# Gated cross-attention block with 64 routed experts: five of eight token groups' experts computed by slots instead of densely, and a new order of the attention's PE work

## The chip, the cores and the metric

The kernel runs on one core of a Trainium2 chip, in fp32. The metric is the device time of one execution in microseconds (us). The engines are PE (TensorE: matmuls and transposes, results in PSUM), DVE (VectorE), ACT (ScalarE), POOL (GpSimd, which also issues the indirect DMAs) and SP (which issues nearly all other DMAs).

## The reference

`x` is 32 batches of 128 tokens of 128 features; a context of the same shape goes with it. First a gated attention with 16 heads of 8 features is added to `x`, then a mixture of 64 experts:

```python
x = x + tanh(g_xattn) * xattn(layernorm(x), ctx)
x = x + tanh(g_ffn) * ffn(layernorm(x))

# xattn: self-attention (kind 0) and attention to ctx (kind 1), both from the queries of x
dots = einsum('bhqd,bhkd->bhqk', q, k) * scale          # scale = 1/sqrt(8)
out  = softmax(dots) @ v * (1 - gate) + softmax(dots_aux) @ va * gate
return out @ Wo + bo

# ffn: per token, 8 of 64 experts
scores = sigmoid(x @ gate_w.T); sc = scores + gate_bias
# the best 4 of 8 groups of experts by the sum of their two best sc, then the best 8 experts in them
tw = scores[chosen] / sum(scores[chosen]) * 2.5
for every expert e:   y += w_dense[:, e] * ((silu(x @ We_gate[e]) * (x @ We_up[e])) @ We_down[e])
return y + (silu(x @ Ws_gate) * (x @ Ws_up)) @ Ws_down
```

The weight of an expert that a token has not chosen is zero. Each expert has 64 hidden features.

## The kernel before

**Units and blocks.** A unit `u` is one batch with one kind of attention: 64 units. A block is 4 batches (512 tokens): 8 blocks. All expert weights stay in SBUF.

**Attention.** `prepare(a)` makes, for two batches, the normalized and transposed inputs (`tp`, `srcT`), queries and keys (`pp`, `qk`), a masked copy of each for pairs of heads (`bd`, on POOL) and the values (`vp`, `v`). For each unit, `scores_max` computes scores `sp` on PE and their negative row maxima `nm` on DVE; `queries` transposes the maxima (`nt`) and adds them to the queries (`qa`); `softmax` computes the scores a second time, transposed and shifted (`st`), and takes their exponential on ACT (`pt`); `values` multiplies with the values (`op`) and copies to `osb`. `divide` (`ot`, `rd`, `at`) and `project` (`mt`, `yp`) finish a batch. `ln_scales` gets the layer norm's inverse root by three Newton steps on DVE (L288 to L295).

**Routing.** When a block's four batches are done, `route(t)` normalizes, transposes (`xtp`, `xT`), computes the gate's scores (`lg`, `sc`), selects groups and experts on DVE, and writes the block's 64 x 512 weights transposed to DRAM (`w_dram`). It is a generator that is advanced a few steps a unit (`route_some`).

**Experts, all dense.** `pair()` takes the next pair of experts of a routed block. There are 33 a block: 32 pairs and the shared expert. `hidden(t, n)` multiplies the block's 512 tokens with gate and up weights of both experts (`gu`, two products of 128x128 with 512 columns), takes silu by Tanh on ACT and two DVE instructions (`th`), and scales by the token weights on POOL (`h`); the weights `cw` are read from DRAM, broadcast over 64 partitions, two pairs in one tile. `down` accumulates `y` over the 33 pairs in one PSUM bank, LAG = 3 pairs behind; after the last, `ysb`, `yt` add the block's sum to `x` and it is stored.

**Order.** A loop over units issues the work: `queries(u-1)`, `scores_max(u)`, a pair, `project`, `divide`, `softmax(u-1)`, a pair, a routing step, `values(u-2)`, a pair, a routing step, a pair. The tile scheduler then orders each engine's instructions; `softmax` is placed before other waiting work by `high_priority` but behind the pair's `down` (`BEHIND`). What is left of the pairs follows the loop. PSUM's eight banks: three double banks (`ps_s`) shared by `sp`, `st` and `gu`, one for everything else, one for `y`.

Of the kernel before, what the change touches and what calls it, by code (L numbers as in the profile page):

```python
# [13 lines left out]
I32 = mybir.dt.int32  # L14
AF = mybir.ActivationFunctionType
# [6 lines left out]
P = 128  # L22
# [4 lines left out]
BG = 4  # L27
# [4 lines left out]
PQ = 2  # L32
AHEAD = 60
LAG = 3
# [3 lines left out]
MAGIC = float(0x5F3759DF)  # L38
BIG = 3.0e38
EPS = 1e-5  # L40


@with_exitstack
def gated_block_kernel(
# [81 lines left out]
    wg_sb = keep.tile([P, E, F], F32, name="wg_sb")  # L126
    wu_sb = keep.tile([P, E, F], F32, name="wu_sb")
    wd_sb = keep.tile([P, NPAIR, D], F32, name="wd_sb")
    wsg_sb = keep.tile([P, F], F32, name="wsg_sb")
    wsu_sb = keep.tile([P, F], F32, name="wsu_sb")  # L130
    wsd_sb = keep.tile([F, D], F32, name="wsd_sb")

    def load_experts(e0):
        e1, p0 = e0 + 8, e0 // 2
        yield nc.sync.dma_start(
            out=wg_sb[:, e0:e1, :], in_=We_gate[e0:e1].rearrange("e d f -> d e f")
        )
        yield nc.sync.dma_start(
            out=wu_sb[:, e0:e1, :], in_=We_up[e0:e1].rearrange("e d f -> d e f")
        )  # L140
        yield nc.sync.dma_start(
            out=wd_sb[:, p0 : p0 + 4, :],
            in_=We_down[e0:e1].rearrange("(p e) f d -> (e f) p d", e=2),
        )

    def load_shared():
        yield nc.sync.dma_start(out=wsg_sb, in_=Ws_gate)
        yield nc.sync.dma_start(out=wsu_sb, in_=Ws_up)
        yield nc.sync.dma_start(out=wsd_sb, in_=Ws_down)

    weight_loads = [partial(load_experts, e0) for e0 in range(0, E, 8)] + [load_shared]

# [4 lines left out]
    nc.gpsimd.memset(one, 1.0)  # L157

# [9 lines left out]
        channel_multiplier=0,  # L168
    )
# [106 lines left out]
    def ln_stats(src, mv):  # L276
        st = work.tile([P, V.BN_STATS_DIM], F32, tag="bnst", name="bnst", bufs=4)
        V.bn_stats(st, src)
        V.bn_aggr(mv, st)

    def ln_scales(mv, n, name):


        var, rs, nr, mr = (
            work.tile([P, n], F32, tag=f"{k}{n}", name=f"{k}_{name}")
            for k in ("var", "rs", "nr", "mr")
        )
        V.tensor_scalar(var, mv[:, :, 1], EPS, None, ALU.add)  # L288
        V.tensor_scalar(rs.bitcast(I32), var.bitcast(I32), -0.5, MAGIC, ALU.mult, ALU.add)
        for _ in range(3):  # L290
            V.tensor_tensor(nr, rs, rs, ALU.mult)
            V.tensor_tensor(nr, nr, var, ALU.mult)
            V.tensor_scalar(nr, nr, -0.5, 1.5, ALU.mult, ALU.add)
            V.tensor_tensor(rs, rs, nr, ALU.mult)
        V.scalar_tensor_tensor(mr, mv[:, :, 0], -1.0, rs, ALU.mult, ALU.mult)  # L295
        return rs, mr
# [6 lines left out]
    fix = ctx.enter_context(tc.tile_pool(name="fix", bufs=1))  # L303
    lp = ctx.enter_context(tc.tile_pool(name="lp", bufs=2))
    work = ctx.enter_context(tc.tile_pool(name="work", bufs=2))
    rt = ctx.enter_context(tc.tile_pool(name="rt", bufs=1))
    hp = ctx.enter_context(tc.tile_pool(name="hp", bufs=2))

    ps_s = ctx.enter_context(tc.tile_pool(name="ps_s", bufs=3, space=PSUM))
# [9 lines left out]

    def share_banks():  # L320

        early.close()
        ps_m.append(ctx.enter_context(tc.tile_pool(name="ps_m1", bufs=1, space=PSUM)))
        ps_y.append(ctx.enter_context(tc.tile_pool(name="ps_y", bufs=1, space=PSUM)))
# [19 lines left out]
    def prepare(a):  # L344
# [16 lines left out]
        srcT = lp.tile([P, 2, AG * S], F32, tag="srcT", name=f"srcT{a}")  # L361
# [8 lines left out]
        bds = [lp.tile([P, 2, 2, AG * S], F32, tag=f"bd{n}", name=f"bd{a}_{n}") for n in range(3)]  # L370
        for n, kind in enumerate((0, 0, 1)):
# [9 lines left out]
            for r in range(2):  # L381
                nc.scalar.activation(  # L382
                    qkk[n][:, r], pp[:, r], AF.Identity, bias=bcol[:, n, r : r + 1]
                )
                for j in range(2):
                    nc.gpsimd.tensor_scalar(  # L386
                        bds[n][:, r, j, :], qkk[n][:, r], mask[:, j : j + 1], None, ALU.mult
                    )
# [18 lines left out]
    def unit_parts(u):  # L407
# [3 lines left out]
        return b, kind, i, qkk[0], qkk[1 + kind], vs[:, kind], bds[0], bds[1 + kind]  # L411

    nm_of = {}
    reached = {}

    def scores_max(u):
# [4 lines left out]
        for r in range(2):  # L421
            for g in range(4):
                p0 = g * SLOT
                mm = nc.tensor.matmul(  # L424
                    sp[g // 2][:, g % 2, 2 * r : 2 * r + 2, :],
                    q[p0 : p0 + MX, r, ts(i, S)],
                    kbd[p0 : p0 + MX, r, :, ts(i, S)],
                    start=True,
                    stop=True,
                )  # L430
        reached[u] = mm.ins.name
        for gp in range(2):
            V.tensor_reduce(  # L433
# [6 lines left out]
        nm_of[u] = nm  # L440

    qa_of = {}

    def queries(u):
# [4 lines left out]
        for n in range(4):  # L449
            nc.tensor.transpose(nt[:, ts(n, S)], nm[:, n].rearrange("p g e -> p (g e)"), ident)  # L450
# [4 lines left out]
            qbd[:, :, :, ts(i, S)],  # L455
            ALU.add,
        )
        qa_of[u] = qa

# [29 lines left out]
    def values(u):  # L489
# [4 lines left out]
        for r in range(2):  # L494
            for j in range(2):
                for g in range(4):
                    nc.tensor.matmul(  # L497
                        op[g * SLOT : (g + 1) * SLOT, r],
                        v[:, i, g, 2 * r + j, :],
                        pt[g // 2][:, g % 2, 2 * r + j, :],  # L500
                        start=j == 0,
                        stop=j == 1,
                    )
# [3 lines left out]
        return osb_of.pop(b) if kind else None  # L507
# [33 lines left out]

    xT = {}

    def route(t):
# [7 lines left out]
        xn = new([BG, D], "xn2")  # L552
# [7 lines left out]
        xt = rt.tile([P, TB], F32, tag="xT", name=f"xT{t}", bufs=2)  # L560
        xT[t] = xt
        nc.scalar.copy(xt, tp)
        yield
# [17 lines left out]
        yield  # L581
# [17 lines left out]
        yield  # L599
# [7 lines left out]
        V.tensor_tensor(v, v, gm.unsqueeze(2).to_broadcast([P, G, E // NG]), ALU.mult)  # L607
        V.tensor_tensor(v, v, pen.unsqueeze(2).to_broadcast([P, G, E // NG]), ALU.add)
        yield
        sel = new([BG, E], "sel")  # L610
        for i in range(BG):
            top = rt.tile([P, TOPK], F32, tag="top", name=f"top{t}_{i}", bufs=4)
            V.max(top, sb[:, i, :])
            V.match_replace(sel[:, i, :], top, sb[:, i, :], -3.3e38)
            if i % 2:
                yield
        V.tensor_tensor(sel, sel, sb, ALU.not_equal)  # L617
        tw = new([BG, E], "tw")
# [3 lines left out]
        yield  # L622
# [3 lines left out]
        V.tensor_scalar(tw, tw, HALF * ROUTE_SCALE, None, ALU.mult)  # L626
        yield
        wp = bank(f"wp{t}")
        for i in range(BG):
            nc.tensor.transpose(wp[0:E, ts(i, P)], tw[:, i, :], ident)  # L630
        wT = rt.tile([E, TB], F32, tag="wT", name=f"wT{t}")
        nc.scalar.copy(wT, wp[0:E, :])
        nc.sync.dma_start(out=w_dram[t], in_=wT)
        load_weights(t, 0)
# [13 lines left out]
    def hidden(t, n):  # L648
# [6 lines left out]
        gu = banks(f"gu{t}_{n}")  # L655
        for i, (wr, ws) in enumerate(((wg_sb, wsg_sb), (wu_sb, wsu_sb))):
            lhsT = wr[:, 2 * n : 2 * n + 2, :].rearrange("p e f -> p (e f)") if n < NPAIR else ws
            nc.tensor.matmul(gu[0:m, i], lhsT, xT[t], start=True, stop=True)  # L658
        th = hp.tile([P, TB], F32, tag="th", name=f"th{t}_{n}", bufs=3)
        nc.scalar.activation(th[0:m], gu[0:m, 0], AF.Tanh, scale=HALF)  # L660
        V.scalar_tensor_tensor(th[0:m], th[0:m], 1.0, gu[0:m, 0], ALU.add, ALU.mult)  # L661
        V.tensor_tensor(th[0:m], gu[0:m, 1], th[0:m], ALU.mult)  # L662
        h = hp.tile([P, TB], F32, tag="h", name=f"h{t}_{n}", bufs=LAG + 1)
        if n < NPAIR:
# [7 lines left out]
    def down(t, n, h):  # L672

        if n == 0:
            sums[t] = ps_y[0].tile([P, TB], F32, tag="y", name=f"y{t}")
        mm = nc.tensor.matmul(  # L676
            sums[t],
            wd_sb[:, n, :] if n < NPAIR else wsd_sb,
# [4 lines left out]
        if n < NPAIR:  # L683
            return mm.ins.name
        ysb = hp.tile([P, TB], F32, tag="th", name=f"ysb{t}", bufs=3)
# [13 lines left out]
        return mm.ins.name  # L699

    waiting = []
    todo = [(t, n) for t in range(NBLK) for n in range(NPAIR + 1)]
    routed = 0

    def pair():
# [4 lines left out]
        waiting.append((t, n, hidden(t, n)))  # L710
        if len(waiting) > LAG:
            return down(*waiting.pop(0))
        return None
# [17 lines left out]

    for u in range(NU + 4):
        if 1 <= u <= len(weight_loads):
# [4 lines left out]
        if 0 <= u - 1 < NU:  # L738
            queries(u - 1)
        if u < NU:  # L740
            scores_max(u)
        done = pair()
        if mixed is not None:
            project(*mixed)
            if mixed[0] % BG == BG - 1:
                routing = route(started)
                started += 1
            mixed = None
        if got is not None:
            mixed = (got[0], divide(*got))  # L750
            got = None
        next(steps, None)
        if 0 <= u - 1 < NU:
            softmax(u - 1, done)
        pair()
        next(steps, None)
        route_some(2 if routed else 4)
        if 0 <= u - 2 < NU:
            osb = values(u - 2)
            if osb is not None:  # L760
                got = ((u - 2) // 2, osb)
        pair()
# [62 lines left out]
```

## Time and profile before

| | |
|---|---|
| time, median of 3 runs | 1224.92 us (1224.64 to 1225.78) |
| profiled execution, its own time | 1226.42 us |
| its span, first to last instruction | 1224.7 us |
| mean granted TensorE clock | 0.96 |
| DMA | 82.73 MB, mean 68 GB/s |
| first `h` of a pair | at 152.8 us |
| last `sp` of the attention | at 1017.6 us |

Busy time is the time in which an engine had at least one instruction running; PE's weight loads (PEld) are listed apart from its matmuls, with which they overlap. An fp32 matmul shows as two instructions of each kind, a transpose as one. A group's row gives line, engine, operation, output and inputs, shapes and count, then busy us and mean ns of one, then the idle time of the engine just before and what ended most of it. The chain of waits follows the run backwards from its last instruction, at each step to what released it.

### The profile page before, as it was taken

What the parts mean: (1) busy time and instruction counts of PE and PEld (TensorE: products, weight loads), DVE (VectorE), ACT (ScalarE), POOL (GpSimd) and SP (SyncE); (2) the same over time, 40 slices, a digit from 0 to 9 for tenths busy, and PEclk for the clock granted to TensorE, in tenths of its full rate; (3) what the DMA queues carried; (4) which work ended last, traced back from release to release, by engine and by line L of the source; (5) the groups of instructions that cost most, each with busy time, mean ns of one, the idle gap of its engine ahead of it and who ended that gap; (6) DMA issues with size and microseconds to landing.
All of it is one profiled execution on the core that took longest, in us unless ns stands there. A gap on an engine that the chain in (4) does not pass through costs nothing.

```text
span 1224.7 us, 17958 instructions
## 1 busy us (share of the span) xinstructions
PE 1146.6 (94%) x6816; PEld 596.4 (49%) x6816; DVE 772.2 (63%) x1685; ACT 413.4 (34%) x732; POOL 518.1 (42%) x480
## 2 busy tenths in 40 slices
PE   3999799998999899999999899998999999999998
PEld 2565455544455454544545454554545444443443
DVE  4365647586466946577665966568575875586554
ACT  2354233332333243343333333342333333222221
POOL 4533063532345253443526244452636233444443
PEclk9698799997899999999999999999999999999999
DMA  3440132210422114212222123212222113334331
GB/s 106 105 115 6 36 76 70 73 35 5 99 73 54 52 26 113 73 53 56 57 80 71 37 56 82 73 53 63 63 63 67 52 52 90 86 79 108 94 104 43
DMA packets 73138, 82.73 MB, mean 68 GB/s; under 512 B 22490, under 2 KB 39772, under 8 KB 73052
## 3 DMA queue, kind: packets, MB, share of 16 engines
q1 hardware_dynamic: 71536, 80.86, 25.5%
q8 instruction: 53, 0.87, 0.3%
q10 hardware_dynamic: 1516, 0.73, 0.2%
q14 instruction: 33, 0.27, 0.1%
HBM read 78.43 MB, written 3.15 MB: 67 GB/s over the span
## 4 chain that ended last, share of the span: by engine, by line
PE 73%; DVE 20%; ACT 2%; DMA 2%; POOL 1%; issue 1%; POOLq 0%; SPq 0%; ACTq 0%; DVEq 0%
PE gu L658 32%; PE y L676 15%; PE st L472 6%; PE sp L424 4%; PE op L497 4%; PE pp L374 4%; DVE th L661 3%; DVE th L662 3%; PE nt L450 2%; DVE nm L433 2%; PE mt L531 2%; PE ot L513 1%; DVE sc L571 1%; ACT xn L299 1%; DVE sel L617 1%
## 5 line engine op out<-in xcount | busy, mean ns | idle before, releaser
L665 POOL TENSOR_TENSOR h<-th,cw 128x512 f32<-128x512 f32 x256 | 325.5, 1273 | 582.2 <-DVE th L662 427.7
L661 DVE SCALAR_TENSOR_TENSOR th<-th,gu 128x512 f32<-128x512 f32 (+1 forms) x264 | 180.8, 685 | 291.1 <-ACT th L660 290.5
L660 ACT ACTIVATE th<-gu 128x512 f32<-128x512 f32 (+1 forms) x264 | 157.5, 597 | 490.2 <-PE gu L658 462.1
L658 PE MATMUL gu<-xT,wg_sb 128*128 128x512 f32 x512 | 275.5, 620 | 17.3 <-DVE th L662 17.3
L658 PE MATMUL gu<-xT,wu_sb 128*128 128x512 f32 x512 | 266.9, 603 | 0.0
L676 PE MATMUL y<-h,wd_sb 128*128 128x512 f32 x512 | 265.6, 601 | 0.0
L386 POOL TENSOR_SCALAR bd<-qk,mask 128x256 f32<-128x256 f32 x192 | 173.8, 924 | 87.3 <-ACT qk L382 87.3
L662 DVE TENSOR_TENSOR th<-gu,th 128x512 f32<-128x512 f32 (+1 forms) x264 | 182.1, 690 | 7.4
L484 ACT ACTIVATE pt<-st 128x1024 f32<-128x1024 f32 x128 | 130.9, 1024 | 149.5 <-PE st L472 79.2
L433 DVE TENSOR_REDUCE nm<-sp 128x8 f32<-128x1024 f32 x128 | 150.7, 1217 | 23.6 <-PE sp L424 23.6
L676 PEld LDWEIGHTS y<-h,wd_sb 128*128 128x128 f32 x512 | 94.7, 192 | 107.2 <-issue 91.5
L658 PEld LDWEIGHTS gu<-xT,wu_sb 128*128 128x128 f32 x512 | 95.5, 193 | 101.7 <-issue 101.2
L658 PEld LDWEIGHTS gu<-xT,wg_sb 128*128 128x128 f32 x512 | 86.5, 192 | 91.8 <-issue 48.6
L424 PE MATMUL sp<-bd,qk 16*128 16x256 f32 x1024 | 89.7, 424 | 9.1 <-POOL bd L386 7.6
L472 PE MATMUL st<-qa,qk 17*128 17x256 f32 x1024 | 88.4, 426 | 0.7 <-DVE nm L433 0.4
L497 PE MATMUL op<-pt,v 128*32 128x128 f32 x2048 | 72.1, 283 | 11.0 <-DVE at L518 10.3
L497 PEld LDWEIGHTS op<-pt,v 128*32 128x32 f32 x2048 | 54.2, 113 | 55.9 <-issue 17.4
L472 PEld LDWEIGHTS st<-qa,qk 17*128 17x128 f32 x1024 | 53.5, 195 | 46.6 <-DVE nm L433 30.6
L424 PEld LDWEIGHTS sp<-bd,qk 16*128 16x128 f32 x1024 | 52.5, 193 | 29.6 <-issue 13.8
L452 DVE TENSOR_TENSOR qa<-nt,bd 128x512 f32<-128x512 f32 x64 | 43.7, 682 | 31.0 <-PE nt L450 30.9
L382 ACT ACTIVATE qk<-pp,bcol 128x256 f32<-128x256 f32 x96 | 40.3, 471 | 58.2 <-PE pp L374 58.0
L374 PE MATMUL pp<-srcT,wpad 128*128 128x256 f32 x192 | 59.4, 439 | 0.5 <-ACT srcT L366 0.5
(135 smaller groups left out, 749.5 us busy)
## 6 DMA issues: line engine op xcount, KB each, us to landing
cw<-w_dram SPq DMA_DIRECT2D x256, 256.0 KB, 4.0
x<-in_x_dram SPq DMA_DIRECT2D x8, 256.0 KB, 4.0
ctx<-in_ctx_dram SPq DMA_DIRECT2D x16, 128.0 KB, 3.8
wg_sb<-in_L_ffn_We_gate_dram SPq DMA_DIRECT2D x8, 256.0 KB, 2.9
wu_sb<-in_L_ffn_We_up_dram SPq DMA_DIRECT2D x8, 256.0 KB, 3.5
wd_sb<-in_L_ffn_We_down_dram SPq DMA_DIRECT2D x8, 256.0 KB, 3.7
out_dram<-x SPq DMA_DIRECT2D x8, 256.0 KB, 2.2
w_dram<-wT SPq DMA_DIRECT2D x8, 128.0 KB, 2.3
```

The source lines that it names most:

```text
L386: nc.gpsimd.tensor_scalar(bds[n][:, r, j, :], qkk[n][:, r], mask[:, j : j + 1], None, ALU.mult)
L424: mm = nc.tensor.matmul(sp[g // 2][:, g % 2, 2 * r : 2 * r + 2, :], q[p0 : p0 + MX, r, ts(i, S)], kbd[p0 : p0 + MX, r, :, ts(i, S)], start ...
L433: V.tensor_reduce(nm[:, :, 2 * gp : 2 * gp + 2, MX].rearrange("p b g -> p g b"), sp[gp], AX.X, ALU.max, negate=True,)
L472: mm = nc.tensor.matmul(st[g // 2][:, g % 2, 2 * r : 2 * r + 2, :], k[p0 : p0 + MX + 1, r, ts(i, S)], qa[p0 : p0 + MX + 1, r], start=True, ...
L484: nc.scalar.activation(pt, st[gp], AF.Exp, scale=1.0 / math.sqrt(DH))
L497: nc.tensor.matmul(op[g * SLOT : (g + 1) * SLOT, r], v[:, i, g, 2 * r + j, :], pt[g // 2][:, g % 2, 2 * r + j, :], start=j == 0, stop=j == 1,)
L658: nc.tensor.matmul(gu[0:m, i], lhsT, xT[t], start=True, stop=True)
L660: nc.scalar.activation(th[0:m], gu[0:m, 0], AF.Tanh, scale=HALF)
L661: V.scalar_tensor_tensor(th[0:m], th[0:m], 1.0, gu[0:m, 0], ALU.add, ALU.mult)
L662: V.tensor_tensor(th[0:m], gu[0:m, 1], th[0:m], ALU.mult)
L665: nc.gpsimd.tensor_tensor(h, th, cws[t, n // PQ][:, n % PQ, :], ALU.mult)
L676: mm = nc.tensor.matmul(sums[t], wd_sb[:, n, :] if n < NPAIR else wsd_sb, h if n < NPAIR else h[0:F], start=n == 0, stop=n == NPAIR,)
```

## The change

Only blocks 0 and 1 (their pairs are mixed into the attention) and block 7 (at the end) keep dense experts. Blocks 2 to 6 are computed by slots, in two rounds of three and two blocks (`ROUNDS`).

- **Slots.** For each sparse block, `route` counts the tokens of every expert on PE (`pos`: products with a triangular matrix `before` and with `ones`) and gives each expert tiles of 128 slots. Each chosen (token, expert) gets a slot number (`place`); a table of the expert of each tile (`table`) is made at the end of a round. NT is the number of tiles: 160 in the first round, 128 in the second.
- **Scatter.** For each batch and each of a token's 8 choices, one indirect DMA from POOL writes 128 rows of 512 bytes into `xslot` in DRAM, 32 DMAs a block. `xslot` is cleared before in 36 stores of 512 KB.
- **Quads.** After the attention its SBUF and PSUM are given back, `We_down` is loaded a second time by expert, and in an order written by hand (`manual_schedule`) quads of four tiles run: load, transpose, `gu` with the tile's own expert, whose number PE reads from `table` into a register (`value_load`, with a bound check), silu (now one ACT instruction), product, transpose, `y`, store to `yslot`. The shared expert of a block is a quad of its own kind.
- **Combine.** For each batch, 8 indirect DMAs from POOL gather the rows of `yslot`; DVE scales them by the token's shares and adds them to `x`. The first round's combines run beside the second round's quads, the second's beside block 7's dense pairs.
- **Routing of block 7** runs beside the quads.
- **Attention.** `values(u-2)` stands between `scores_max(u)` and `softmax(u-1)`; all three are put behind what was issued before. One pair a unit, two while the pairs are behind; seven (`LEFT`) are left for after the loop. `ln_scales` takes a power on POOL. `bd` tiles are for one batch each.
- Dense pairs: `cw` for one pair a tile (PQ = 1), LAG = 2; block 7's pairs use Silu and scale on DVE.

The core of the diff, with what the prediction speaks of:

```diff
-PQ = 2
+S0 = 2
+ROUNDS = (3, 2)
+QT = 4
+LEFT = 7
+PQ = 1
-LAG = 3
+LAG = 2
...
+    NT = [-(-(n * TB * TOPK // P + E - 1) // QT) * QT for n in ROUNDS]
...
-        V.tensor_scalar(var, mv[:, :, 1], EPS, None, ALU.add)
-        V.tensor_scalar(rs.bitcast(I32), var.bitcast(I32), -0.5, MAGIC, ALU.mult, ALU.add)
-        for _ in range(3):
-            V.tensor_tensor(nr, rs, rs, ALU.mult)
-            V.tensor_tensor(nr, nr, var, ALU.mult)
-            V.tensor_scalar(nr, nr, -0.5, 1.5, ALU.mult, ALU.add)
-            V.tensor_tensor(rs, rs, nr, ALU.mult)
+        nc.gpsimd.tensor_scalar(rs, mv[:, :, 1], EPS, None, ALU.add)
+        nc.gpsimd.tensor_tensor(rs, rs, mhalf[:, 0:n], ALU.pow)
...
+        def scatter(i, r, after):
+            k = nc.gpsimd.indirect_dma_start(
+                out=xslot[c],
+                out_offset=IndirectOffsetOnAxis(ap=place[c][:, i0 + i, r : r + 1], axis=0),
+                in_=xn[:, i, :],
+                in_offset=None,
+            ).ins
...
+        if t >= S1:
+            nc.scalar.activation(th[0:m], gu[0], AF.Silu)
+            if n < NPAIR:
+                V.tensor_tensor(th, th, cws[t, n // PQ][:, n % PQ, :], ALU.mult)
+            pace[0] = V.tensor_tensor(h[0:m], gu[1], th[0:m], ALU.mult).ins.name
+            return h
...
         if u < NU:
-            scores_max(u)
+            scores_max(u, done if ps_y else None)
         done = pair()
+        new = None
+        if 0 <= u - 2 < NU:
+            done, new = values(u - 2, done)
+        if 0 <= u - 1 < NU:
+            softmax(u - 1, done if ps_y else None)
+        if u < NU:
+            scatter_some(3, paced[u])
...
+        if behind() > 0:
+            pair()
+        scatter_some(2, pace[0])
...
+        def experts(name, xt, wgu, wd):
+
+            gu = ps_g.tile([P, QT, 2, F], F32, tag="g", name=f"gu{name}")
+            for n in range(QT):
+                nc.tensor.matmul(gu[:, n], xt[:, ts(n, P)], wgu[n], start=True, stop=True)
+                if n % 2:
+                    some_number()
+            h = qp.tile([P, QT, F], F32, tag="h", name=f"h{name}")
+            nc.scalar.activation(h, gu[:, :, 0, :], AF.Silu)
+            pace[0] = V.tensor_tensor(h, h, gu[:, :, 1, :], ALU.mult).ins.name
+            yield
+            ht = ps_h.tile([P, 512], F32, tag="h", name=f"ht{name}")
+            for n in range(QT):
+                nc.tensor.transpose(ht[0:F, ts(n, P)], h[:, n, :], ident)
+            hts = qp.tile([F, 512], F32, tag="hts", name=f"hts{name}")
+            V.tensor_copy(hts, ht[0:F, :])
+            yield
+            y = ps_q.tile([P, QT * D], F32, tag="y", name=f"y{name}")
+            for n in range(QT):
+                nc.tensor.matmul(y[:, ts(n, D)], hts[:, ts(n, P)], wd[n], start=True, stop=True)
+                if n % 2:
+                    some_number()
+            return y
...
+            def number(n):
+                a, b = divmod(q * QT + n, P)
+                e.append(
+                    nc.tensor.value_load(table[c][0:1, a, b : b + 1], min_val=0, max_val=E - 1)
+                )
...
+            for r in range(TOPK):
+                k = nc.gpsimd.indirect_dma_start(
+                    out=yg[:, r, :],
+                    out_offset=None,
+                    in_=yslot[c],
+                    in_offset=IndirectOffsetOnAxis(ap=place[c][:, i, r : r + 1], axis=0),
+                ).ins
+                tc.add_manual_dep(k, pace[0], AFTER)
+                if r % 2:
+                    yield
+            V.tensor_tensor(
+                yg, yg, shares[c][:, i].unsqueeze(2).to_broadcast([P, TOPK, D]), ALU.mult
+            )
...
+        for c in range(len(ROUNDS)):
+            shared_out = weights(c)
+            for n, _ in enumerate(every_quad(c)):
+                advance(last)
+                advance(shared_out)
+                advance(back, 1 + n % 2)
...
+            back = chain(back, every_combine(c))
+        routed = NBLK
+        while advance(back) | bool(todo):
+            pair(two)
```

## The prediction

> **What bounds the kernel now.** I read the page's busy times and slices first, then the chain of waits for what a step costs on the path, then windows by stage, last the groups and DMA issues for prices.
>
> ```profile
> PE 1146.6 (94%) x6816; PEld 596.4 (49%) x6816; DVE 772.2 (63%) x1685; ACT 413.4 (34%) x732; POOL 518.1 (42%) x480
> ...
> PE   3999799998999899999999899998999999999998
> ...
> PEclk9698799997899999999999999999999999999999
> ```
>
> TensorE is busy almost to the end and nobody else is; its granted clock is full after the first fifth. So the time is TensorE's work plus what it loses. The chain of waits around 600 us and near the end gives prices of whole steps (start, us, step):
>
> ```profile
> 607.29 0.31 PE yp L537 x2
> ...
> 608.46 0.89 PE vp L394 x8
> 609.35 0.86 PE y L676 x2
> 610.21 1.01 PE op L497 x32
> ...
> 618.26 0.44 PE nt L450 x4
> 618.70 1.08 PE sp L424 x16
> ...
> 1191.99 1.72 PE gu L658 x4
> 1193.70 0.86 PE y L676 x2
> ```
>
> An expert pair is gu 1.72 + y 0.86 = 2.58 us, and 8 blocks x 33 pairs x 2.58 = 681 us: over half of the run. A 128-column fp32 product is two instructions of 111 ns (vp: 0.89/8), a 128x128 transpose one of 110 ns (nt: 0.44/4). The stages by windows (PE, PEld, DVE, ACT, POOL busy, clock, DMA share, GB/s):
>
> ```profile
> 54.00:115.00 61.00, 57.83 (x713) 40.74 (x712) 37.74 (x85) 31.62 (x55) 25.93 (x29) 0.94 0.29 72
> ...
> 150.00:1017.00 867.00, 834.36 (x5192) 431.80 (x5195) 569.28 (x1224) 307.89 (x544) 376.23 (x338) 0.98 0.24 63
> ...
> 1040.00:1214.00 174.00, 170.79 (x479) 76.02 (x478) 105.31 (x192) 43.11 (x76) 79.25 (x62) 0.99 0.35 90
> ```
>
> Attention without experts, attention with experts (50 units in 867 us, 17.3 us each), experts alone. The prices of the other engines:
>
> ```profile
> L665 POOL TENSOR_TENSOR h<-th,cw 128x512 f32<-128x512 f32 x256 | 325.5, 1273 | 582.2 <-DVE th L662 427.7
> L661 DVE SCALAR_TENSOR_TENSOR th<-th,gu 128x512 f32<-128x512 f32 (+1 forms) x264 | 180.8, 685 | 291.1 <-ACT th L660 290.5
> ...
> L386 POOL TENSOR_SCALAR bd<-qk,mask 128x256 f32<-128x256 f32 x192 | 173.8, 924 | 87.3 <-ACT qk L382 87.3
> ...
> L433 DVE TENSOR_REDUCE nm<-sp 128x8 f32<-128x1024 f32 x128 | 150.7, 1217 | 23.6 <-PE sp L424 23.6
> ...
> cw<-w_dram SPq DMA_DIRECT2D x256, 256.0 KB, 4.0
> ```
>
> **What goes.** 5 of 8 blocks no longer run all 64 experts: 165 pairs x 2.58 = 426 us of TensorE, with 165 x (0.68 + 0.69) = 226 us of DVE and 165 x 1.27 = 210 us of POOL. The Newton steps of L288 to L294 (69 us on DVE over the run, summed from their groups) become two POOL instructions.
>
> **What comes, stage by stage.**
>
> *Attention with 59 pairs (66 less LEFT).* Per unit the PE needs nt, sp, st, op = 3.6; half of ot 0.59, mt 0.64, yp 0.31 = 0.8; a quarter of tp, six pp and vp (0.44 + 6 x 0.43 + 0.89; two pp take 0.87 in the same chain) = 1.0; an eighth of routing = 0.2: 5.6 us. Fourteen units are done by 140 us before (counted from the nm rows); I keep that start, as routing must end before the first pair can begin. Some 15 new memsets and iotas at the start, 0.1 to 0.4 us each by the rows of their kind, stand on POOL, which the chain passes before the first scores (its bd rows); about 2 us, which the earlier finish of the first batch's bd by the new order gives back. The other 50 units carry 57 pairs, 2.9 us each unit, with 0.1 for the slot counts: 8.6 us of PE. DVE: nm 2.4, qa 0.7, halves and quarters 1.0, routing 1.4, the new slot arithmetic (about 9 us a block, from rows of 0.17 to 0.42) 0.7, pair 1.14 x 1.37 = 1.6: 7.7 us. POOL: bd 12 x 0.92/4 = 2.8, h 1.14 x 1.27 = 1.4, and from about unit 29 the scatters, 160 in 38 units, 4.2 a unit. Three engines are thus close to each other, where before only one was loaded.
>
> The scatter's price has no row. From below: the issue of cw holds SP 0.6 us (median of its row) and the landing, 4.0 us, is not waited for by the next issue. [...] Without scatters I take 9.2 a unit (8.6 at somewhat better than the 90% that the stage reaches now), with them 9.7: 140 + 15 x 9.2 + 35 x 9.7 + 12 for the last units = 630 us. [...] Moving op between sp and st gives DVE 1.0 us more for nm (2.4 us): without it st would wait; I count it within the 9.2. The clears (36 x 512 KB) and xT, key stores go through SP behind cw loads; with a pair every 8 us cw has time. Five blocks' cw loads (8 MB each: 256 issues of 256 KB over 8) vanish, the others come in twice as many issues.
>
> *Between the stages.* 7 pairs at 2.58 and their drain, 20 us, hiding the 2 MB of wd_sb.
>
> *Slots.* NT is 160 and 128 tiles: 72 quads. PE per quad: 4 transposes x 0.11, gu and y two instructions a product, 16 x 0.111, 4 transposes of h with half the columns to load, 0.075: 0.44 + 1.78 + 0.3 = 2.5 us. [...] ACT per quad: silu near 0.4, two copies at the srcT group's 0.58: 1.6. DVE: 0.4 + 0.6, plus weights and combine near 1. Both below PE, and covered by it. A combine's multiply waits on DVE for its eight gathers with h and hts of the quads queued behind it, and so PE; as it is issued three combines after them, this shows only where POOL falls behind the loop. On SP a quad's store waits for its ysb copy with the next loads behind it; they are wanted three steps later, 7 us and more against the 4 us of the cw and x loads. Transfers: 512 KB a quad and, in the second round, 2.4 gathers of 64 KB; the windows give 72/0.29 = 248 GB/s at a full share, so 2.1 and 2.7 us.
>
> The four expert numbers are read by PE's own sequencer. No row shows a register load. Below: hidden behind queued matmuls, 0. [...] They are spread between matmuls, so part is hidden: I take 3.4 us. 72 x 3.4 + 5 shared quads x 2.5 + 15 for two fills, drains and activation tables (1.28 each in the before) = 272 us. If the cover goes, each 0.1 us per number costs 29 us.
>
> *Last block.* 33 x 2.58 = 85, 3 to start, 12 for the last combines and stores: 100. [...]
>
> Sum 630 + 20 + 272 + 100 = 1022, against the profiled execution's own 1226.4 (span 1224.7 and 1.7 around it); that run lies 1.5 us above the median of 1224.9. I predict 1020.
>
> **Rivals.**
> 1. *Everything hides.* Numbers behind matmuls, scatters under 1 us: 50 units at 8.8 = 440, so 592; 18; quads at the transfer floor of 2.7 = 195 + 27; 97: 930. For it: SP's 0.6 us. Against: three engines between 7.7 and 9 us a unit, in one order.
> [...]
> 3. *Number loads stall PE.* At 1.0 us each, serial, a quad is 6.5 and the sum 1245; from 0.94 us it loses.
> That the tile scheduler undoes the new order between the score passes is possible too; it moves a unit by under 1 us, within my range.
>
> **How the numbers follow.** My forecast 0.63, the first rival 0.18, the second 0.12 (0.05 of it beyond 1.93 us), the third 0.06 (0.03 beyond 0.94), no change 0.01. Faster 0.91, within 0.2% (about what a measurement of this kernel can tell from no change) 0.01, slower 0.08. Attention 9.0 to 10.5 a unit and quads 2.9 to 4.5 put my own case at 960 to 1100. The range must reach into the first rival and the milder half of the second and third: 890 to 1170.
>
> **What would show it.** Right: attention ending near 630 us with POOL near 90% busy from 280 us on and PE near 90%; indirect DMAs about 1.2 us apart where POOL has nothing else; quads every 3.4 us with PE's gaps at register loads; a gapless last block. Wrong: quads 5 us or more apart, DVE waiting for gathers in the second round or the last block, or attention units over 11 us.

## The result and the profile after

The changed kernel takes 1479.78 us (median of 4 runs, 1472.37 to 1483.55) against 1224.78 us for the kernel before on the same chip: a ratio of 1.207, with a 95% interval of 1.203 to 1.212. The forecast was 1020 us, in a range of 890 to 1170. The profiled execution took 1483.55 us, with a span of 1481.8 and a mean granted clock of 0.825 (before 0.96).

First from its page: TensorE's busy time, its busy share and its granted clock by slices.

```profile
PE 1153.7 (78%) x7652; PEld 723.7 (49%) x7652; DVE 702.7 (47%) x1511; ACT 421.9 (28%) x779; POOL 620.0 (42%) x666
...
PE   3997798777777778777777878838888877888995
...
PEclk9688899899787676879778777868999878877998
```

The row to stop at is the first: TensorE is busy for 1153.7 us, though 165 of 264 pairs are gone. Before it was 1146.6. The two rows below say how: nearly every slice is 7 or 8 where it was 9, and the clock goes down to 6 and 7 where it had been 9. The same product takes longer, and between products TensorE waits. By windows (us, busy time of PE, PEld, DVE, ACT, POOL, clock, DMA share, GB/s): the attention from the first scatters on, the two rounds of slots, the last block.

```profile
431.00:955.00 524.00, 397.71 (x2832) 221.61 (x2833) 250.39 (x602) 140.32 (x253) 263.14 (x274) 0.77 0.16 53
...
985.00:1163.00 178.00, 146.48 (x925) 116.58 (x925) 74.00 (x155) 61.09 (x117) 9.54 (x10) 0.92 0.40 113
1163.00:1370.00 207.00, 163.82 (x913) 136.30 (x913) 90.34 (x164) 52.71 (x106) 99.81 (x96) 0.78 0.47 129
1370.00:1460.00 90.00, 85.49 (x188) 36.23 (x187) 53.92 (x86) 17.80 (x30) 59.85 (x57) 0.96 0.49 134
```

In the attention no engine is the bound: PE is busy 76%, POOL 50%, DVE 48%. The attention's last `qa` starts at 936.3 us, against 1033.1 before. The forecast's stages against these:

| stage | forecast, us | measured, us |
|---|---|---|
| attention | 630 | 936 |
| between | 20 | 49 |
| slots | 272 | 385 |
| last block | 100 | 112 |

The attention is counted here to its last `qa`, the slots from 985 us, the last block from 1370 us. 306 of the 460 us by which the forecast missed lie in the attention and 113 in the slots.

What a unit does with its time is seen in the timeline of one (start, us, engine, line, operation; in brackets the idle time of that engine just before and what ended it):

```profile
602.33 1.11 PE L511 MATMUL nt<-ident,nm 128*128 128x128 f32 x4 [0.93 <-ACT qk L434]
603.37 2.09 PE L482 MATMUL sp<-bd,qk 16*128 16x256 f32 x16
...
605.39 3.78 PE L868 MATMUL gu<-xT,wgu_sb 128*128 128x512 f32 x4
...
609.11 1.08 PE L562 MATMUL op<-pt,v 128*32 128x128 f32 x32
...
610.12 1.15 PE L536 MATMUL st<-qa,qk 17*128 17x256 f32 x16
...
612.35 0.37 ACT L573 COPY osb<-op 128x256 f32<-128x256 f32 x1 [2.48 <-PE st L536]
...
612.78 0.71 PE L598 MATMUL mt<-ident,at 128*128 128x128 f32 x4 [1.51 <-ACT osb L573]
...
614.78 0.49 PE L604 MATMUL yp<-wo_sb,msb 128*128 128x128 f32 x2 [0.43 <-ACT msb L602]
...
615.65 1.16 PE L451 MATMUL vp<-wv_sb,srcT 128*128 128x128 f32 x8 [0.38 <-DVE x L605]
...
618.96 0.86 PE L511 MATMUL nt<-ident,nm 128*128 128x128 f32 x4 [2.15 <-ACT v L461]
```

From `nt` to the next `nt` are 16.6 us with one pair's `gu` in them. Two things are to be seen. `nt`, `op`, `mt`, `yp` and `vp` all use the one bank `m`: each waits until ACT or DVE has emptied it for the one before (0.93 us before `nt`, 1.51 before `mt`, 2.15 before the next `nt`). And at a low clock, 0.57 from 602 to 610 us, the work itself swells: `nt` 1.11 us, `sp` 2.09 and `gu` 3.78, where timelines at full clock show 0.60, 1.15 and 1.88. (A timeline counts each group some 0.1 us longer than the chain of waits, from which the forecast's 0.44, 1.08 and 1.72 come.) Later in the same unit the clock is back, 1.00 from 610 to 619 us, and `st` takes 1.15.

### The profile page after: what moved, and what is told of

Same layout as the page of the kernel before. It is cut to its first block, busy times and chain, and to the rows that moved or that the text cites. A ratio compares the mean times of both kernels' runs of the same rounds, so it can differ in the third digit from the quotient of the medians.

```text
span 1481.8 us, 21670 instructions
## 1 busy us (share of the span) xinstructions
PE 1153.7 (78%) x7652; PEld 723.7 (49%) x7652; DVE 702.7 (47%) x1511; ACT 421.9 (28%) x779; POOL 620.0 (42%) x666
## 3 DMA queue, kind: packets, MB, share of 16 engines
q8 instruction: 66, 1.08, 0.3%
## 5 line engine op out<-in xcount | busy, mean ns | idle before, releaser
L1156 POOL DMA_INDIRECT yg<-yslot,place x160 | 168.5, 1053 | 306.4 <-DMA key<-key_dram 183.9
L868 PE MATMUL gu<-xT,wgu_sb 128*128 128x512 f32 x384 | 238.4, 750 | 4.3 <-issue 2.2
L805 POOL DMA_INDIRECT xslot<-xn,place x160 | 157.3, 983 | 144.1 <-DVE nm L493 58.6
L882 POOL TENSOR_TENSOR h<-th,cw 128x512 f32<-128x512 f32 x64 | 81.5, 1275 | 218.7 <-DVE th L880 72.8
L893 PE MATMUL y<-h,wp_sb 128*128 128x512 f32 x192 | 116.8, 697 | 67.3 <-POOL h L882 67.2
L868 PEld LDWEIGHTS gu<-xT,wgu_sb 128*128 128x128 f32 x384 | 81.8, 232 | 107.0 <-issue 99.8
L878 ACT ACTIVATE th<-gu 128x512 f32<-128x512 f32 (+1 forms) x66 | 39.4, 596 | 320.8 <-PE gu L868 306.2
L1065 PE MATMUL y<-wd_sb,hts 64*128 x576 | 101.8, 315 | 18.4 <-DVE hts L1061 14.8
L1050 PE MATMUL gu<-wgu_sb,xqt 128*128 x576 | 104.1, 321 | 11.3 <-issue 11.2
L1050 PEld LDWEIGHTS gu<-wgu_sb,xqt 128*128 128x128 f32 x576 | 88.5, 225 | 22.1 <-issue 21.3
```

What stands on the lines that cost most here:

```text
L805: k = nc.gpsimd.indirect_dma_start(out=xslot[c], out_offset=IndirectOffsetOnAxis(ap=place[c][:, i0 + i, r : r + 1], axis=0), in_=xn[:, i, ...
L868: mm = nc.tensor.matmul(gu[i], lhsT, xT[t], start=True, stop=True)
L882: nc.gpsimd.tensor_tensor(h, th, cws[t, n // PQ][:, n % PQ, :], ALU.mult)
L893: nc.tensor.matmul(sums[t], wp_sb[:, n, :] if n < NPAIR else wsd_sb, h if n < NPAIR else h[0:F], start=n == 0, stop=n == NPAIR,)
L1050: nc.tensor.matmul(gu[:, n], xt[:, ts(n, P)], wgu[n], start=True, stop=True)
L1065: nc.tensor.matmul(y[:, ts(n, D)], hts[:, ts(n, P)], wd[n], start=True, stop=True)
```

## The experiments

The units' length below is the mean from the 17th `qa` to the 64th, 47 units. It was 17.4 us in the kernel before and 15.5 in the changed one.

**1. What does a pair in the attention cost?** The forecast said 2.58 us of TensorE each. First the changed kernel with the pairs held back until the attention is over, with one bank as before (e2) and with two banks for the small products all through (e1; the second bank is given up only when the pairs begin).

```diff
-        if not todo or todo[0][0] >= routed:
+        if hold or not todo or todo[0][0] >= routed:     # e1, e2; cleared after the loop
...
-                if routed == 1:
-                    share_banks()                        # e1: called after the loop
```

> The changed kernel, with all 66 dense pairs of blocks 0 and 1 held back until the attention is over, and the small products of the attention keeping two PSUM banks to its end (the y bank is made only then). Theory (a unit's own chain through one PSUM bank and in-order queues sets about 15 us a unit in the changed kernel; dense pairs only filled its gaps): with two banks and no pairs a unit falls to 6.5 to 8 us, as in the first units before any pair, attention ends near 520 us, then 66 x 2.6 = 172 us of pairs, then the 495 us that the slots, the last block and the ends take now: about 1190 us. Rival (new order of sp, op and st holds PE): the order stays, so a unit stays at 12 us or more: over 1450. Rival (scatters on POOL): units without scatters near 7, those with 12 or more: about 1350.

> As the run with held pairs, but the small products go down to one PSUM bank when the first block is routed, as in the changed kernel. Theory with the bank as its main part: a unit stays at 11 to 14 us from there on, attention ends near 850 us and the whole takes about 1500. If instead the pair and its DVE and ACT work between the score passes lengthen the chain, the units fall as with two banks: about 1200.

e1 took 1348.08 us, ratio 1.104 (1.099 to 1.109): last `qa` at 685.0, 10.6 us a unit, so the 6.5 to 8 us expected with two banks were not reached. (That the time fits the last rival's 1350 is luck: its units without scatters were to take 7 us and took 9.2.) e2 took 1541.6 us: last `qa` at 882.9, 14.3 us a unit without a single pair. So of the attention's 936 us only some 50 were the pairs'. More pairs, then: four dense blocks with up to three pairs a unit (e8), five with up to four (e11), and seven, which is the change without any slots (e13; block 7 is then routed after the attention, before its pairs). The three edits are written as one here.

```diff
-S0 = 2
-ROUNDS = (3, 2)
+S0 = 4                 # e11: 5      e13: 7
+ROUNDS = (2, 1)        # e11: (2,)   e13: ()
...
-        if behind() > 0:
-            pair()
+        for _ in range(2):      # e11, e13: 3
+            if behind() > 0:
+                pair()
```

> The changed kernel with four dense blocks mixed into the attention and three by slots (two and one), up to three pairs a unit: 66 more pairs in the attention, 16 quads and 64 scatters less. Theory (pairs fill gaps that are there anyway): the attention ends within 50 us of 955, the slots take about 80 us less and fewer scatters give some 40 back: 1340 to 1400. Rival (each pair lengthens its unit by its PE time): attention past 1100, run over 1480.

> Five blocks dense in the attention instead of two, up to four pairs a unit, and two blocks by slots in one round of 128 tiles; the last block dense at the end as before. 99 more dense pairs in the attention (255 us of TensorE at full clock), 160 fewer tiles, 96 fewer scatters and gathers. If pairs fill idle gaps and hold the clock up: attention's last qa at 930 to 980 with a clock of 0.95 or more, slots 32 quads and 2 shared ones at 4.2 us plus fill 160, last block 110: 1200 to 1270 us in all, near the kernel before. If pairs cost TensorE time in the attention as the prediction summed (2.58 each): last qa at 936 + 255 less 80 for the scatters, 1110, and 1400 in all.

> The changed kernel without slots: seven blocks dense in the attention with up to four pairs a unit, the eighth at the end, everything else of the change kept (order of the score passes, power on POOL, one pair a cw tile, Silu in the last block). It parts the change in two. If the slots and what comes with them are the whole loss: attention's last qa at 1005 to 1030 with a clock near 1.0 and 1210 to 1240 us in all, the kernel before within 1.5%. If the new order also costs (the 20 us in the attention that the old order saved): 1240 to 1280. If it gains what the prediction gave it (nm no longer waited for, under 1 us a unit): 1170 to 1210.

| | pairs before the last `qa` | last `qa`, us | us a unit | whole run, us |
|---|---|---|---|---|
| e2 | 0 | 882.9 | 14.3 | 1541.6 |
| changed | 59 | 936.3 | 15.5 | 1479.78 |
| e8 | 125 | 931.9 | 15.4 | 1373.95 |
| e11 | 158 | 1002.3 | 16.7 | 1322.96 |
| e13 | 197 | 1032.2 | 17.2 | 1245.1 |
| before | 200 | 1033.1 | 17.4 | 1224.78 |

The pairs are counted from the `gu` instructions of the traces; those left over run after the attention. From 200 pairs to 59 the attention falls by 97 us: 0.7 us a pair, not 2.58. Those are whole kernels, and with the pairs the scatters change too (none in e13, 160 in the changed kernel and in e2). Where the scatters are equal, a pair costs more: 0.9 us from e2 to the changed kernel (53 us for 59 pairs), and 1.25 us from e4 below to e13, neither of which has scatters (172 us for 138 pairs). So a pair here costs a third to a half of its own time. The attention of e11 (ratio of the whole 1.083, 1.077 to 1.088) is longer than the 930 to 980 us expected from gaps alone. e13 (1.018, 1.013 to 1.022) shows that without slots all the rest of the change leaves the attention where it was, within 1 us. And the more blocks are dense, the faster the whole. What e13 loses is at its end, which takes 210 us from the last `qa` where it took 192: block 7's routing, which before ran beside the pairs left over, now stands alone behind them (the chain of waits of e13, start, us, step):

```profile
1146.01 0.44 DVE both L730
1146.47 0.30 DVE both L732
1146.91 1.05 PE wp L736 x4
1147.98 0.59 ACT wT L738
1148.59 2.23 DMA w_dram<-wT
...
1151.39 3.18 DMA cw<-w_dram
```

**2. Bank or clock?** e2's windows show a second cause beside the bank: TensorE stood at half its clock (0.50), and was busy 80% of the time only because of it. e9 and e12 add products that nobody reads to e2, in the bank of `y`, which lies idle there: three pairs of gate/up products a unit (e9), then two (e12).

```diff
+        ft = ps_y[-1].tile([P, TB], F32, tag="y", name=f"fill{u}_{n}")
+        for i in range(2):
+            nc.tensor.matmul(ft, wgu_sb[:, i, 2*n : 2*n+2, :].rearrange("p e f -> p (e f)"),
+                             xT[0], start=True, stop=True)
```

> The changed kernel with all 66 dense pairs held back until the attention is over and one bank for the small products (as in e2, where the clock stood at 0.50 and a unit took about 14 us), plus three pairs of gate/up products a unit that nobody reads, in the otherwise idle y bank: 5.2 us of TensorE a unit at full clock, about 270 us over 52 units. Bank theory (one bank and in-order queues set the unit, the clock only follows): units stay at 14 us or grow, last qa at 883 us (e2) or later, up to 1000. Clock theory (the unit is long because TensorE idles and is then granted half its clock): granted clock in the attention over 0.8, units of 9 to 12 us, last qa at 700 to 800 although 270 us of work were added. Pure addition, no slack at all: last qa near 1150.

> As e9 (pairs held back, one bank m, unread products in the idle y bank), but two pairs of such products a unit instead of three, 4.4 us of TensorE a unit instead of 6.6. In e9 TensorE was 93% busy, so the unit of 12.5 us there may be the filler's own. Clock theory with a short chain: granted clock 0.85 or more and units of 10 to 11 us, last qa at 720 to 780. Clock theory with a threshold above this load: clock 0.55 to 0.75, units 12.5 to 14, last qa 810 to 880. Bank theory (at full clock the chain through m still takes 12 us or more): clock near 0.9 and units of 12 to 13, last qa 800 to 830.

The windows from 200 to 850 us of e2 and e9, then those of e12 from 200 to 330, and the filler's group in e9:

```profile
200.00:850.00 650.00, 519.90 (x3704) 345.06 (x3704) 265.20 (x670) 172.64 (x315) 255.66 (x286) 0.50 0.12 42
```

```profile
200.00:850.00 650.00, 598.95 (x4556) 338.05 (x4555) 293.28 (x776) 185.29 (x337) 278.30 (x309) 0.96 0.15 51
```

```profile
200.00:330.00 130.00, 121.63 (x1088) 74.39 (x1084) 61.68 (x135) 47.84 (x88) 37.89 (x46) 1.00 0.18 60
```

```profile
L961 PE MATMUL fill<-xT,wgu_sb 128*128 128x512 f32 x668 | 343.6, 627 | 1.0 <-ACT wT L738 0.7
```

The filler's 668 instructions are 287 us of TensorE at the 0.43 us that `gu` has at full clock (1.72 for four); the group's busy time of 343.6 overlaps its neighbours. This useless work made the attention 71 us shorter: last `qa` at 811.9 instead of 882.9, 12.9 us a unit, with a clock of 0.96 instead of 0.50. That is what the clock theory had said in kind, though it had hoped for 700 to 800. In e9 TensorE is busy 92%, so the filler itself is now the bound. e12 shows what the chain through one bank can do at full clock: in units 17 to 28 it takes 10.9 us a unit, with TensorE busy 94%. The forecast's 5.6 and 2 x 1.72 of filler would be 9.0; the 6.6 and 4.4 us of filler in the expectation for e12 came from busy times and were too high. The same units of e2 take 14.2 us, so at least 3.3 of them were the clock's. Later e12 is disturbed (below), so that its last `qa` comes at 806.1; whole runs 1484.19 us (e9) and 1508.01 (e12), as the pairs still follow.

That the bank matters too is e1's part: 10.6 us a unit at a clock of only 0.74 (200 to 650 us). Giving the small products three banks, and scores and `gu` two double banks instead of three, was tried with the changed kernel's pairs (e10) and with all dense (e14).

```diff
-    ps_s = banked.enter_context(tc.tile_pool(name="ps_s", bufs=3, space=PSUM))
+    ps_s = banked.enter_context(tc.tile_pool(name="ps_s", bufs=2, space=PSUM))
...
-        ps_m.append(banked.enter_context(tc.tile_pool(name="ps_m1", bufs=1, space=PSUM)))
+        ps_m.append(banked.enter_context(tc.tile_pool(name="ps_m1", bufs=3, space=PSUM)))
```

> The changed kernel, with the double banks for scores and gate/up products cut from three to two and the bank of the small products raised from one to three. Bank theory, in the form that the single bank m is what chains a unit: units fall from 16.5 to 10 to 12 us, last qa near 700 to 750. If it is the sequence of the unit's steps as issued, with any shared bank taking the place of m: sp must then wait for the pair's gu to be read and st for sp, units stay at 15 to 18 us, last qa 900 to 1000. Clock theory: no direct effect, last qa within 30 us of 936 with a clock near 0.77.

> As e13, with two double banks instead of three for scores and gate/up products and three banks m instead of one (e10's edit). With TensorE busy 94% there is little for more banks to give: if they close the rest, units of 16 to 16.5 us and 1160 to 1200 in all; if gu now waits for the scores' maxima more often (80 us of such waits in e10), 1230 to 1300.

e10 took 1374.02 us, last `qa` at 877.4: 59 us less, with a clock of 0.87 from 431 us on, between the forms in which bank and sequence had been expected. e14 took 1374.62, ratio 1.124 (1.118 to 1.130), 19.2 us a unit. With four pairs a unit the third double bank is worth more than two banks `m` (17.2 us a unit in e13, which has it). Both expectations for e14 were too low.

e5 doubles the gate/up products of blocks 0 and 1, so that each takes twice its time in the place where it stands.

```diff
+            for _ in range(2 if t < S0 else 1):
                 mm = nc.tensor.matmul(gu[i], lhsT, xT[t], start=True, stop=True)
```

> The changed kernel with each gate and up product of blocks 0 and 1 issued twice into the same place: 66 x 1.72 = 114 us more of PE work in the attention at the full clock, nothing else. Theory (PE waits out the chain of a unit; what is put into the gaps costs nothing, and keeps the granted clock up): the run stays within 30 us of the changed kernel's 1480, or gets shorter. Rival (PE's work sets the unit): 1590 or more.

1552.58 us, ratio 1.268 (1.261 to 1.276), last `qa` at 1008.5. Neither theory nor rival holds: of the 101 us added before the last `qa` (59 pairs), 72 come out there. Work put into the gaps is thus not free as such. One reading is that the place counts: e9's filler has no consumer, while `gu` stands in the chain of a unit between `sp` and `op`, which are put behind it. Another is that e2's clock of 0.50 left more to win than the changed kernel's. The runs do not part the two.

**3. Order, scatters, power, numbers.** e3 gives back the order of before between the score passes; e4 leaves the scatters out (the slots hold zeros); e6 takes Newton's steps on DVE instead of the power on POOL; e7 gives each tile a fixed expert instead of the one read from the table. Of e3 and e6 only one line is shown; e3 also puts `softmax` and `values` back behind the pair.

```diff
-            scores_max(u, done if ps_y else None)       # e3: order of the kernel before
+            scores_max(u, None)
...
-            f, *a = to_scatter.pop(0)                   # e4
-            f(*a, after)
+            to_scatter.pop(0)
...
-        nc.gpsimd.tensor_tensor(rs, rs, mhalf[:, 0:n], ALU.pow)   # e6: three Newton steps on V
...
-                e.append(
-                    nc.tensor.value_load(table[c][0:1, a, b : b + 1], min_val=0, max_val=E - 1)
-                )
+                e.append((q * QT + n) % E)              # e7
```

> The changed kernel with the order of the attention's issue as before: scores_max without a place of its own, a pair, project and divide, softmax behind the pair, then values. Theory (chain, unfilled): units stay at 13 to 16 us, whole run 1420 to 1540. Rival (the new order holds PE): units fall to about 10 us, whole run near 1150 to 1200.

> The changed kernel without its 160 scatters (the slots then hold zeros only); all else stays. Theory (chain): the units from the 29th on shorten by at most 1 to 2 us where a scatter stands before h or the power on POOL: 1400 to 1450. Rival (POOL's scatters are the bound): they fall from 16 to below 12 us: 1300 or less.

> The changed kernel with the layer norm's inverse root by Newton steps on DVE as before, instead of the power on POOL. The run without scatters was 140 us shorter. Theory (the scatters hurt where something waits behind them on POOL: the power, whose result ACT's queue waits for with the copies of v and msb behind it): 40 to 100 us shorter, 1380 to 1440. Rival (the scatters hurt by h and bd, or by the POOL time itself): within 20 us of 1480.

> The changed kernel with expert numbers fixed when the program is built instead of read into PE registers (tiles then use a wrong expert). Quads of the first round now come every 4.3 us, of which PE works 3.7. Theory (number loads are the gaps between the groups of a quad): a quad falls to 3.5 to 3.7 us, the slots lose 45 to 60 us: about 1425. Rival (the gaps are waits for ACT and DVE): quads stay above 4.1 us, run within 15 us of 1480.

- e3: 1417.83 us, last `qa` at 916.1. The new order costs 20 us in this attention. Both orders lie far above the forecast.
- e4: 1339.96 us, last `qa` at 859.9, between theory and rival. The scatters cost 76 us of the attention. The changed kernel shows it within one run too: its units take 13.9 us before the first scatter (at 431 us) and 16.3 behind it. It is not their issue time: POOL is only half busy (254 of 505 us). From about there to the last `qa` the changed kernel and then e4, without scatters, run as many instructions on TensorE, 2710:

```profile
431.00:936.00 505.00, 379.50 (x2710) 211.68 (x2710) 240.34 (x574) 134.83 (x243) 254.17 (x265) 0.77 0.15 51
...
424.00:860.00 436.00, 333.99 (x2710) 190.70 (x2710) 237.80 (x576) 136.42 (x243) 127.67 (x136) 0.86 0.12 40
```

  Of the 69 us between them, 45 are the same products at a lower clock and 24 are idle time of TensorE, about as much as its waits for `osb`, 22.3 us, which e4 does not have. What holds `osb`, and why the clock falls further, is not shown; in e2, whose clock is at 0.50 anyway, a unit takes 14.3 us before the scatters as behind them. In the changed kernel's list of waits, POOL stands before a scatter until `nm` is there, and the pair's `y` stands behind `h` on POOL (us in total, times, longest; the last line is e4's). The waits for `h` are not much shorter without scatters, only the longest are:

```profile
PEld y L893 <- POOL h L882: 80.4, 40, 12.8
...
PE y L893 <- POOL h L882: 67.2, 35, 11.9
...
POOL xslot L805 <- DVE nm L493: 58.6, 17, 8.3
...
PE y L892 <- POOL h L881: 52.5, 47, 3.8
```

- e6: 1478.9 us, ratio 1.212 (1.207 to 1.216), which is the changed kernel's own. The power is no cause.
- e7: 1424.84 us, as the theory said. The chain of waits in the first round, of the changed kernel and of e7:

```profile
1103.39 1.25 PE y L1065 x8
1104.65 0.21 issue
1104.86 0.62 PE ht L1059 x4
1105.48 1.16 PE gu L1050 x8
1106.64 0.52 issue
1107.16 0.63 PE xq_26t L1104 x4
1107.79 1.25 PE y L1065 x8
```

```profile
1021.31 1.08 PE y L1065 x8
1022.39 0.56 PE ht L1059 x4
1022.95 0.89 PE gu L1050 x8
1023.84 0.44 PE xq_8t L1102 x4
1024.28 1.09 PE y L1065 x8
```

This quad takes 4.40 us with numbers and 2.97 without. In the median of the first round it is 4.28 and 2.97: 0.33 us a number. In e7 TensorE has no gap left, and its groups add up to the quad. In the second round e7 gains only 4 us, as that round is disturbed in both runs (below).

## Why the prediction was wrong

**The step that failed** is "Per unit the PE needs" 5.6 us and the sum of 8.6 us that was then taken "at somewhat better than the 90% that the stage reaches now". Ninety per cent was a property of TensorE being overloaded: in the kernel before, 3.9 pairs a unit filled every wait of the attention's own chain (TensorE busy 834 of 867 us from 150 to 1017 us). Taken out, they left the waits. A unit without pairs takes 14.3 us (e2) at the clock that it then gets, and up to 10.9 at full clock (e12), not 5.6/0.9. Over the 47 units of the changed kernel:

```profile
210.00:936.00 726.00, 552.59 (x4106) 310.45 (x4098) 358.35 (x842) 206.48 (x372) 328.13 (x343) 0.80 0.16 55
```

That is 11.8 us of TensorE a unit where the sum had 8.6, and 3.7 us of waiting where the forecast had 0.6 to 1.1. So both terms were too small: 3.2 us more work, most of it by the clock (8.6/0.80 is 10.8), and some 3 us more waiting. For the scatters it had 0.5 us a unit; the trace shows 2.3.

Two signs stood in the trace of before. The first units, without pairs and with two banks, took 5 to 10 us from `qa` to `qa`, 7 in the mean, not 5.6. And the clock was not "full after the first fifth": the tenth and eleventh slices of the row that the prediction shows, from 276 to 337 us, are 7 and 8. There block 0's pairs had run out and block 1 was not yet routed, so that no pair's `gu` was issued from 284 to 311 us:

```profile
284.00:311.00 27.00, 25.89 (x134) 14.76 (x135) 10.65 (x17) 6.46 (x11) 8.63 (x9) 0.62 0.02 6
```

**The clock** was in no case of the forecast. All its durations came from stages with a clock of 0.94 or more and were kept for a TensorE with half the work. At half clock throughout, the 0.50 of e2, 8.6 us a unit would have been 17 and the attention 140 + 50 x 17 = 990 us instead of 630. That this lies near the measured 936 is luck: the clock was 0.80, and the rest is waiting. The low clock did not come with long gaps of TensorE: in e2, from 200 to 850 us, only four gaps were above 1.4 us (3.7 us each, four routing steps), and the clock was 0.50 all through. Filling the short waits with products brought it back (0.96 in e9 from 200 to 850 us, 1.00 in e12 from 200 to 330). What it answers to, the waits or the small products beside them, these runs do not part; but from 54 to 115 us, where the small products run without pairs and almost without waits (TensorE busy 95 and 96%), the clock was 0.94 in the kernel before and 0.82 in the changed one, not 0.50.

**Point by point.**
- *165 pairs x 2.58 = 426 us.* By TensorE's time at full clock right, as a saving wrong: the 141 pairs that left the attention, 364 us of TensorE, made it 97 us shorter.
- *Scatter 1.2 us.* No row of before shows the 1.2 us. The price was good all the same: the runs show 0.96 to 0.98 us each, 1.26 apart back to back. The groups (busy us, mean ns | idle before and why):

```profile
L805 POOL DMA_INDIRECT xslot<-xn,place x160 | 157.3, 983 | 144.1 <-DVE nm L493 58.6
...
L1156 POOL DMA_INDIRECT yg<-yslot,place x160 | 168.5, 1053 | 306.4 <-DMA key<-key_dram 183.9
```

  The 1.93 us that stands with the second rival's chance was not reached, and POOL was not the bound: it was busy 50% from 431 to 955 us. But LAG = 2 did not cover an `h` behind scatters on POOL: `y` waits for `h` up to 12.8 us, and even without scatters LAG does not cover it (52.5 us in e4).
- *Moving `op` between `sp` and `st`.* Counted as a small gain; e3 shows a loss of 20 us here, e13 no effect with all blocks dense.
- *Power on POOL.* No cause: e6, without it, took 1478.9 us.
- *Quad 3.4 us.* It takes 4.28 in the first round (median). No run shows the 0.9 us that it adds for four numbers to the 2.5 us of TensorE; the runs show 1.31 (4.28 less the 2.97 of e7), 0.33 us a number. The 2.5 us of TensorE measured 2.97 even in e7; of the difference, 0.26 is `ht`, 0.56 us where 0.3 was taken. Without numbers the quads of the first round would be below the forecast. Beside the gathers and combines of the second round the quad is 5.4 in the changed kernel, but 4.3 in six other runs (below).
- *Between the stages 20 us.* 49. The attention's own end takes 19 of it (last `yp` at 955.0 us), and `y` waits 11.9 us for an `h` that stands behind scatters on POOL.
- *Last block 100 us.* 112; the only stage that came out as worked out, with TensorE busy 95%.
- *Third rival, numbers from 0.94 us.* Wrong in size.

One thing stays open. From the first to the last `y` of the quads it is 363 us in the changed kernel, and 358, 360 and 362 in e5, e6 and e12, but 324 to 327 in e1, e2, e3, e4, e9 and e10, which have the same quads. All of it lies in the second round: the first takes 169 to 171 us in all ten, the second 159 to 169 in the four and 133 or 134 in the six, at a clock of 0.97 to 1.00. In the four, this round or its start has stalls of 5 us and more that the profile puts down to no known queue, and a clock of 0.80 to 0.88; in the six there is no such stall. No edit sorts the two groups, but the chip does: e1 to e4 ran on one, e9 and e10 on a second, e5 and e6 on a third, e12 on a fourth. Which one the changed kernel ran on is not known, and no edit was run on two of them, so the cause is not shown. Some 35 us of the whole difference are thus not explained by the change, and whole runs of the two groups are apart by as much before any edit counts. The changed kernel has no such stall in its attention, so that the comparisons of last `qa` are free of it.

No kernel here beats the one before. The nearest is e13, the change without its slots.

## What to carry to other kernels

Before taking work off a busy engine, work out the length of the chain that remains without it, buffers and queues included (here `y` waited 11.9 us for an `h` behind scatters on POOL), and at the clock that TensorE will then have: the freed time is at most the difference between the present step and that chain. Dense filler in another stage's waits can cost far less than its own time (here 0.7 to 1.25 us for 2.58 us of work), and TensorE's clock was 0.96 with filler (e9) where it was 0.50 without (e2). Take such work away where it stands alone, not where it hides.

## What was not expected of the hardware

TensorE's clock stayed at 0.50 for 650 us although its queue was busy 80% of the time, and 287 us of useless products made the same stage 71 us shorter.

In e12, four units took 23.7 to 28.2 us. In the timeline of one, TensorE deals out the last of `op` and all of `st` in ones to fives over some 15 us, with gaps in which it waits for nothing shown, while POOL issues scatters without a break; ACT's copy of `op` waits 20 us:

```profile
490.67 0.79 PE L536 MATMUL st<-qa,qk 17*128 17x256 f32 x2
...
491.93 1.28 PE L536 MATMUL st<-qa,qk 17*128 17x256 f32 x3 [0.47 <-issue]
...
494.02 1.23 PE L536 MATMUL st<-qa,qk 17*128 17x256 f32 x3 [0.82 <-issue]
...
496.15 1.01 PE L536 MATMUL st<-qa,qk 17*128 17x256 f32 x3 [0.90 <-issue]
...
504.73 0.37 ACT L573 COPY osb<-op 128x256 f32<-128x256 f32 x1 [20.34 <-remote]
```

The same 16 instructions take 1.15 us otherwise. What holds TensorE in these gaps is not shown; e9, with the same scatters and on another chip, has no such unit.
